# Two full products of the identity ahead of every second group's scores, in the context attention of the last two sequences

## The chip, the cores and the metric

The kernel runs on one core of a Trainium2 chip, in one launch. The metric is the device time of that launch in microseconds. Three runs of the kernel before gave 906.14, 907.43 and 909.11; the median is 907.43.

Five engines work side by side, each through its own list of instructions in order: TensorE (PE in the profile; its weight loads stand apart as PEld), VectorE (DVE), ScalarE (ACT), GpSimd (POOL) and SyncE (SP), which mostly issues transfers. They wait for each other by semaphores.

## The reference, cut to what matters

A decoder of two layers works on `x` of 4 sequences by 256 tokens by 256 channels. The six parts are added to `x` one after the other: latent attention, an attention over a context, a routed block, an attention over heads, the causal context attention that the change touches, and a mixture of 28 experts of which each token takes six. The part in question, and what follows it:

```python
def _L1_xattn_ref(q, latent_kv, Wq, Wkv_expand, Wout):   # 16 heads of 16
    qp = q @ Wq.T
    kv = latent_kv @ Wkv_expand.T
    k, v = jnp.split(kv, 2, axis=-1)
    ...
    scores = jnp.einsum('bhqd,bhkd->bhqk', qh, kh) * inv_sqrt_d
    scores = jnp.where(causal, scores, jnp.finfo(scores.dtype).min)
    attn = jax.nn.softmax(scores, axis=-1)
    out = jnp.einsum('bhqk,bhkd->bhqd', attn, vh)
    ...
    return out @ Wout.T
...
x = x + _L1_xattn_ref(_layernorm(x, axis=-1), ctx_512, ...)
x = x + _L1_ffn_ref(_layernorm(x, axis=-1), ...)
```

## The kernel before

All data is f32 but for some constants. A kernel-wide PSUM pool has three tags of two buffers each: `sc` (two banks a buffer), `tp` and `o`.

`_cross_attention` handles the sequences in two halves, `half(0)` for sequences 0 and 1 and `half(1)` for sequences 2 and 3. The second half runs alone on the core's engines but for the routing of the experts; the first runs beside the head attention. `front` makes the queries `f["qT"]` of two sequences at once: 128 rows (eight heads of 16, in two interleaved sets), two sets `g`, 512 tokens. A product of 128x512 (`xpq`, L1669) fills each set, and DVE scales it into `xqT` (L1670).

Each sequence `b` then has eight groups of two times one head: `g` (0, 1), `e` (0, 1), `sp` (0, 1). For a group, `scores` (L1545) takes a buffer of `sc` and fills its two banks. Each bank gets a product of 32 rows by 256 keys (`Q1`, the later queries), one of 32 rows by 128 keys (`Q0`), and then a product of the identity in bf16 with the mask (L1559). The first product into a bank is the one with `start=True`. DVE takes the maxima (`cnm`, L1561 and L1562), ACT the exponentials (`xpr`, L1567).

The groups are pipelined: when a group's scores are issued, `after` takes up the group two before it. `turned` transposes its exponentials, six times 128x128 into two `tp` tiles (`x_tp`), which DVE copies out (L1583), or ACT for the last of each four (L1581). With the next group's scores the sums over the values follow (`values`, `xav`: 128 rows by 32 columns, four side by side). After four groups `finish` scales the sums (`xwide` on ACT L1603, `xr_tp` on PE, `xrT` on ACT L1609, `xaT` on DVE L1611), and after eight it projects them (`xpo`, eight records of 128x256) and adds them to `x` (L1623).

Then `env["then"](b)` routes the sequence's tokens: statistics (L143 to L146), the reciprocal root on POOL (`ln_rs`, L135), the normed rows `R` (L151), their transposes `g_tp` (L630) and copy `ghT` (L632), the gate's product `pl` (L637), a chain of small DVE instructions to the chosen experts `gt` (L670), the ranks (`rank`, L677 and L678), the row numbers `rows` (L686), and twelve scatters from POOL into the `lists` in DRAM (L702). Steps of this alternate with the groups of the next sequence. POOL does all this in order: `R`'s clearing (L620) and the `ln_rs` of the next routing stand behind the twelve scatters.

The order of the PE instructions of this part is written out by a helper: `_InOrder` (`pe`) ties each product of line 94 and each transpose of line 97 to the one before it. Where the routing's own PE instructions (`g_tp`, `pl`, `rank`) stand among them, and the order on DVE and ACT, is left to a scheduler, which places them by its own estimates of time. So a change of one product can move others.

When the last `xpo` is done, the memory of this part is free, and the load of the experts' second weights (`wdn_e`, L593) starts into it; the experts follow.

Of the kernel before, what the change touches and what calls it, by code (L numbers as in the profile page):

```python
# [1481 lines left out]
def _cross_attention(nc, tc, x, w, env):  # L1482
# [5 lines left out]
    ident, identb, maskb, ln_apply, transposed = (env[n] for n in ("ident", "identb", "maskb", "ln_apply", "transposed"))  # L1488
    H = D = 16
    pe = _InOrder(nc, tc)  # L1490
# [53 lines left out]

    def scores(f, b, g, e, sp, ss):  # L1545
        sc = psum.tile([P, 2, 512], F32, tag="sc", name="xsc")
        t0 = b % 2 * S
        for cols, q0, n in ((Q1, P, S), (Q0, 0, P)):
            for j in range(2):
                rows = slice(32 * (2 * sp + j), 32 * (2 * sp + j) + 32)  # L1550
                pe.matmul(
                    sc[:, j, cols],
                    f["qT"][rows, g, t0 + q0 : t0 + q0 + P],
                    f["kz"][rows, e, g, t0 : t0 + n],
                    start=(n == S),
                    stop=False,
                )
        for j in range(2):
            pe.matmul(sc[:, j, P : 3 * P], identb, masks, start=False, stop=True)  # L1559
        nm = sm.tile([P, 2, 2], F32, tag="cnm", name="cnm")  # L1560
        nc.vector.tensor_reduce(nm[:, 1], sc[:, :, Q1], AX.X, ALU.max, negate=True)  # L1561
        nc.vector.tensor_reduce(nm[:, 0], sc[:, :, Q0], AX.X, ALU.max, negate=True)  # L1562
        pr = c3.tile([P, 2, 3 * P], F32, tag="xpr", name="xpr")
        for j in range(2):
            h = 8 * g + 2 * (2 * sp + j) + e
            for i, cols in ((1, Q1), (0, Q0)):
                nc.scalar.activation(  # L1567
                    pr[:, j, cols], sc[:, j, cols], AF.Exp, bias=nm[:, i, j : j + 1], accum_out=ss[:, i, h : h + 1]
                )
        return pr  # L1570
# [103 lines left out]
    def half(bp):  # L1674
        while bp not in kvs:
            yield
        f = yield from front(bp, kvs[bp])
        for b in (2 * bp, 2 * bp + 1):
            ss = c2.tile([P, 2, H], F32, tag="xss2", name="xss2")
            for n in range(8):  # L1680
                g, e, sp = n // 4, n // 2 % 2, n % 2
                now = (f, b, g, e, sp, scores(f, b, g, e, sp, ss), ss)
                yield
                advance()
                waiting.append(now)
                if len(waiting) > 2:
                    after(*waiting.pop(0))
                if b == B - 1:
                    advance()
                yield  # L1690
        if bp == 1:
            while waiting:
                after(*waiting.pop(0))
            state.pop("values")()
            while steps:
                advance()
# [121 lines left out]
```

## Time and profile before

| | us |
|---|---|
| median of three runs | 907.43 |
| the profiled execution | 933.27 |
| its span, first to last instruction | 931.5 |
| mean granted TensorE clock over the span | 0.837 of full speed |
| context attention of sequences 2 and 3, first scores to last `xpo` | 605.2 to 708.7 |
| PE busy in it | 78.6 of 103.5 |
| mean granted clock in it | 0.72 |

A row of the profile gives the busy time of a group of like instructions, and the idle time of its engine just before them with what ended it. A f32 product of the program stands in the trace as two records, a transpose as one. Ends of PE records are modelled. The granted clock (PEclk) is the share of full speed at which the TensorE array runs; the stretches by time give it for any piece of the span. "remote" marks a wait of which the profile finds no releaser among this core's instructions.

### The profile page before, as it was taken

To read this page: it belongs to the slowest core of one execution; us is meant where nothing else is said; L and a number is where in the kernel's file an instruction comes from. 1 tells how busy PE (TensorE), PEld (TensorE's weight loads), DVE (VectorE), ACT (ScalarE), POOL (GpSimd) and SP (SyncE) were. 2 spreads that over 40 slices of the span, in tenths; PEclk is the share of its full clock that TensorE was granted. 3 is DMA by queue.
4 is the path that set the end of the run, shared out by engine and by line. 5 is a ranking of instruction groups with operands and counts; after the bars stand their busy time and mean duration, and the time that the engine had idled before them with its cause. 6 is when DMAs were issued, how large, how long until landed. Compare 5 with 4: busy or idle time off the path is not lost.

```text
span 931.5 us, 11640 instructions
## 1 busy us (share of the span) xinstructions
PE 716.2 (77%) x3634; PEld 447.2 (48%) x3634; DVE 533.2 (57%) x1310; ACT 291.9 (31%) x962; POOL 310.3 (33%) x248
## 2 busy tenths in 40 slices
PE   4998999789988667334857778879665689969990
PEld 2555656445555333322423445556443357747770
DVE  3367457886553599878278579537334233353332
ACT  1245343442441302210322334235220234424440
POOL 2022122213210283440430330231440456645662
PEclk9899989889998588567866778869766799989995
DMA  8779999400515103110400000480124767685655
GB/s 314 206 236 325 325 326 327 180 1 0 181 37 190 47 1 107 73 46 16 137 0 1 1 1 1 184 326 14 64 75 100 230 104 128 111 213 87 112 77 154
DMA packets 85168, 117.83 MB, mean 126 GB/s; under 512 B 5774, under 2 KB 72975, under 8 KB 84594
## 3 DMA queue, kind: packets, MB, share of 16 engines
q1 hardware_dynamic: 72210, 100.26, 33.1%
q0 software_dynamic: 11232, 15.21, 9.7%
q10 hardware_dynamic: 1664, 1.57, 0.5%
q8 instruction: 33, 0.54, 0.2%
q14 instruction: 29, 0.24, 0.1%
HBM read 59.60 MB, written 55.33 MB: 123 GB/s over the span
## 4 chain that ended last, share of the span: by engine, by line
PE 38%; DVE 25%; DMA 14%; POOL 8%; issue 6%; ACT 6%; another core or an unknown queue 1%; SPq 1%; ACTq 0%; DVEq 0%; POOLq 0%
DMA acc<-ys,xb 10%; POOL qk L1412 5%; ACT pr L324 4%; PE xsc L94 3%; PE pgu L848 3%; PE po L94 2%; DVE pv L1437 2%; PE x_tp L97 2%; PE pq L94 2%; DVE s L1418 2%; DVE pr L333 2%; PE pqkv L1394 2%; PE av L94 2%; PE py L879 2%; DVE O L1444 2%
## 5 line engine op out<-in xcount | busy, mean ns | idle before, releaser
L884 POOL DMA_INDIRECT acc<-ys,xb x62 | 98.3, 1586 | 73.6 <-ACT Tx L840 48.0
L1412 POOL TENSOR_TENSOR qk<-qkv 128x1024 f32<-128x1024 f32 x32 | 74.2, 2349 | 92.2 <-ACT qkv L1398 92.2
L848 PE MATMUL pgu<-wgu_e,Tx 128*128 x248 | 90.8, 491 | 8.1 <-issue 6.8
L334 POOL TENSOR_TENSOR pr<-pr,rs 128x512 f32<-128x512 f32 x32 | 41.5, 1297 | 165.0 <-DVE rs L332 78.8
L324 ACT ACTIVATE pr<-sc,nb 128x256 f32<-128x256 f32 x128 | 58.9, 473 | 61.6 <-DVE nb L319 61.5
L1567 ACT ACTIVATE xpr<-xsc,cnm 128x256 f32<-128x256 f32 (+1 forms) x128 | 52.0, 422 | 65.3 <-DVE cnm L1562 50.3
L702 POOL DMA_INDIRECT lists<-R,rows x48 | 46.6, 971 | 59.4 <-DVE rows L686 19.1
L879 PE MATMUL py<-wdn_e,Th 88*128 x248 | 64.3, 385 | 0.8 <-DVE Th L861 0.5
L1418 DVE TENSOR_REDUCE s<-qk 128x128 f32<-128x2048 f32 x16 | 36.5, 2283 | 39.5 <-POOL qk L1412 39.5
L848 PEld LDWEIGHTS pgu<-wgu_e,Tx 128*128 128x128 f32 x248 | 44.3, 199 | 25.4 <-issue 11.1
L879 PEld LDWEIGHTS py<-wdn_e,Th 88*128 88x128 f32 x248 | 47.3, 193 | 17.2 <-DVE Th L861 1.1
L854 DVE TENSOR_TENSOR eh<-pgu,sg 128x176 f32<-128x176 f32 x62 | 21.1, 340 | 53.5 <-issue 31.8
L97 PE MATMUL x_tp<-cst,xpr 128*128 128x128 f32 x192 | 39.7, 345 | 12.5 <-DVE cnt L753 4.3
L94 PE MATMUL av<-pT,ckt 128*64 128x256 f32 x256 | 40.1, 408 | 10.1 <-DVE pT L350 9.9
L315 DVE TENSOR_REDUCE nm<-sc 128x4 f32<-128x1024 f32 x32 | 39.0, 1218 | 14.4 <-PE sc L94 14.3
L852 ACT ACTIVATE sg<-pgu 128x176 f32<-128x176 f32 x62 | 19.7, 317 | 78.4 <-PE pgu L848 68.1
L883 ACT ACTIVATE ys<-py,wsel 128x256 f32<-128x256 f32 x62 | 29.4, 473 | 38.6 <-PE py L879 33.6
L94 PE MATMUL sc<-ckv,qk 64*128 64x256 f32 x256 | 39.9, 413 | 1.5 <-ACT qk L302 0.7
L97 PE MATMUL tp<-cst,pr 128*128 128x128 f32 x256 | 38.1, 290 | 3.3 <-DVE pT L350 2.4
L94 PE MATMUL xsc<-kz,xqT 32*128 32x256 f32 (+1 forms) x256 | 38.5, 412 | 2.7 <-ACT xpr L1567 2.7
L868 DVE SCALAR_TENSOR_TENSOR wjunk<-cst,e_all,xb 128x28 f32<-128x28 f32 x62 | 15.3, 247 | 41.4 <-ACT ys L883 36.7
L97 PEld LDWEIGHTS x_tp<-cst,xpr 128*128 128x128 f32 x192 | 27.6, 176 | 22.0 <-issue 9.0
(339 smaller groups left out, 1523.7 us busy)
## 6 DMA issues: line engine op xcount, KB each, us to landing
lists<-blank SPq DMA_DIRECT2D x9, 3600.0 KB
wgu_e<-in_e_gu_dram SPq DMA_DIRECT2D x4, 2464.0 KB
xb<-lists SPq DMA_DIRECT2D x62, 144.0 KB
acc<-blank SPq DMA_DIRECT2D x5, 1152.0 KB
wdn_e<-in_e_dn_dram SPq DMA_DIRECT2D x4, 1232.0 KB
wq<-in_m_wq_dram SPq DMA_DIRECT2D x4, 1024.0 KB
mwo<-in_m_wo_dram SPq DMA_DIRECT2D x2, 2048.0 KB
part<-acc SPq DMA_DIRECT2D x16, 256.0 KB
```

The lines of the kernel that those rows point to most:

```text
L94: self._next(self.engine.matmul(*args, **kw))
L97: self._next(self.engine.transpose(*args, **kw))
L315: nc.vector.tensor_reduce(nm, sc, AX.X, ALU.max, negate=True)
L324: nc.scalar.activation(pr[:, e, qt, :], sc[:, e, qt, :], AF.Exp, bias=nb[:, e, qt : qt + 1], accum_out=ss[:, e, qt : qt + 1],)
L334: nc.gpsimd.tensor_tensor(pr[:, 1], pr[:, 1], rs[:, 1].unsqueeze(2).to_broadcast([P, 2, S]), ALU.mult)
L702: put = nc.gpsimd.indirect_dma_start(out=lists, out_offset=bass.IndirectOffsetOnAxis(ap=rows[:, i, n : n + 1], axis=0), in_=R[:, i, :], in ...
L848: nc.tensor.matmul(pg, xT[:, k, :], self.wgu[:, bass.ds(e * (4 * M) + k * 2 * M, 2 * M)], start=(k == 0), stop=(k == 1))
L879: nc.tensor.matmul(py, hT[:, k, :], self.wdn[:, bass.ds(e * (2 * C) + k * C, C)], start=(k == 0), stop=(k == 1))
L884: nc.gpsimd.indirect_dma_start(out=accs[self.puts % len(accs)], out_offset=bass.IndirectOffsetOnAxis(ap=xb[:, C : C + 1].bitcast(I32), axi ...
L1412: nc.gpsimd.tensor_tensor(pr[:, 4 * i : 4 * i + 4], q3[:, h0 : h0 + 4].unsqueeze(2).to_broadcast([P, 4, H, D]), k3.unsqueeze(1).to_broadca ...
L1418: nc.vector.tensor_reduce(s[:, hh], pr, AX.X, ALU.add)
L1567: nc.scalar.activation(pr[:, j, cols], sc[:, j, cols], AF.Exp, bias=nm[:, i, j : j + 1], accum_out=ss[:, i, h : h + 1])
```

## The change

Two products are added at the head of `scores`, for sequences 2 and 3 and for the groups with `sp == 0`, so for eight of the sixteen groups. Each multiplies the f32 identity (128x128) with all of `f["qT"][:, 0]` (128x512) and writes one of the two banks of the group's `sc` buffer. The scores' own first product into each bank begins with `start=True`, so that what the added products left there is overwritten and not read.

```diff
     def scores(f, b, g, e, sp, ss):
         sc = psum.tile([P, 2, 512], F32, tag="sc", name="xsc")
+        if b >= 2 and sp == 0:
+
+            for j in range(2):
+                pe.matmul(sc[:, j], ident, f["qT"][:, 0], start=True, stop=True)
         t0 = b % 2 * S
         for cols, q0, n in ((Q1, P, S), (Q0, 0, P)):
             for j in range(2):
```

All lines after it move down by four (L1561 becomes L1565, and so on). The scheduler's order changes in a few places with it. On PE, in the routing of sequence 1, three of the four `rank` products move up, ahead of the sums over the values (`xav`) and of three transposes; in the routing of sequence 2, the four `g_tp` transposes move up, ahead of sixteen `xav` records and six `x_tp`. On DVE a few instructions of these two routings change places with `cnm` and with one reciprocal (L1601), and on ACT one `xwide` comes earlier. POOL's and SP's orders are the same.

## The prediction

> **What bounds the kernel now.** I read the page first, then the stretches by time, then the chain of waits, then the order of time on TensorE and GpSimd. The page:
>
> ```profile
> span 931.5 us, 11640 instructions
> PE 716.2 (77%) x3634; PEld 447.2 (48%) x3634; DVE 533.2 (57%) x1310; ACT 291.9 (31%) x962; POOL 310.3 (33%) x248
> PEclk9899989889998588567866778869766799989995
> ```
>
> No engine is full over the span, and the granted clock has a trough in the middle (slices of 23.3 us each). The products that the change repeats stand at line 94, writing `xsc`; the groups of the last two sequences run from 605.2 to 708.7 us. Cut where the granted clock switches (columns: length, busy time of PE, PEld, DVE, ACT, POOL, then PEclk, DMA share, GB/s):
>
> ```profile
> 605.20:611.00 5.80, 4.05 (x43) 2.65 (x42) 1.71 (x3) 1.72 (x8) 4.30 (x5) 1.00 1.03 408
> 611.00:617.70 6.70, 4.56 (x20) 2.50 (x20) 1.12 (x2) 0.00 (x0) 3.84 (x4) 0.50 1.04 411
> 617.70:631.50 13.80, 12.62 (x56) 8.49 (x54) 6.53 (x14) 8.28 (x36) 0.26 (x3) 0.50 0.48 188
> 631.50:648.20 16.70, 15.49 (x153) 11.60 (x153) 14.25 (x53) 8.53 (x37) 0.72 (x1) 1.00 0.00 1
> 648.20:655.40 7.20, 4.92 (x51) 3.41 (x50) 3.62 (x7) 3.90 (x17) 5.65 (x6) 1.00 0.29 104
> 658.80:665.60 6.80, 2.69 (x22) 1.58 (x20) 1.13 (x3) 1.72 (x9) 3.75 (x7) 1.00 0.28 101
> 665.60:686.10 20.50, 16.90 (x85) 11.71 (x86) 11.43 (x47) 6.34 (x27) 3.38 (x4) 0.50 0.04 16
> 692.90:706.60 13.70, 8.79 (x48) 4.39 (x48) 3.40 (x16) 3.35 (x12) 3.84 (x4) 0.50 0.15 54
> ```
>
> The clock is 1.00 or 0.50 and nothing between. In the full-speed stretch 631.5 to 648.2, PE is busy 15.49 of 16.70 us: there TensorE is the bound, with 1.2 us to spare. Elsewhere it idles. Two things hold the order of the stage. One is GpSimd: each sequence's routing issues twelve scatters (L702), and the next routing's `ln_rs` (L135) is queued on POOL behind them:
>
> ```profile
> 662.24 0.96 POOL L702 DMA_INDIRECT lists<-R,rows  x1 [0.30 <-issue]
> 664.81 0.10 POOL L620 MEMSET R<- 128x6 f32 x1 [1.61 <-DMA lists<-R,rows]
> 668.37 0.72 POOL L135 TENSOR_TENSOR ln_rs<-ln_ve,neghalf 128x2 f32<-128x2 f32 x1 [3.29 <-DVE ln_ve L146]
> ```
>
> The batches start at 648.2 and 682.8 us, and twelve scatters take 12 x 1.265 = 15.2 us. The other thing is PE itself. At the end, the chain of waits runs through the last `xpo` straight into the load of the expert weights, so whatever ends the stage later ends the kernel later:
>
> ```profile
> 707.16 1.51 PE xpo L94 x6
> 708.68 12.05 DMA wdn_e<-in_e_dn_dram
> ```
>
> One feature of the profile needs care. Late in each batch VectorE waits for products that had ended long before, with no releaser found:
>
> ```profile
> DVE cnt L753 <- remote: 7.9, 1, 7.9
> DVE xpT L1583 <- remote: 5.7, 3, 4.4
> DVE x_in L1623 <- remote: 4.0, 1, 4.0
> ```
>
> The profiled execution took 933.27 us (931.5 of span, 1.8 around it); the median is 907.43, shorter by 25.8. These waits, ACT's like them, and another such stretch near 732 to 742 us sum to about that. My inference, not shown: they are mostly absent from the timed runs. So I make the sum twice, with them and without.
>
> **The change part by part.** It adds, before the scores of groups 0, 2, 4, 6 of both sequences, two products of 128*128 by 512 f32: eight pairs. Nothing is removed. The nearest row is the query product of the same shape:
>
> ```profile
> 599.12 6.19 PE L1669 MATMUL xpq<-hT,wxq 128*128 128x512 f32 x8
> ```
>
> Eight records are four program products; they start 0.855 us apart at clock 0.50. A pair is four records: 3.42 us at half clock, 1.71 at full (the scores block beside it takes 2.12 against 1.18). Eight pairs: 13.7 us at full, 27.4 at half. The identity's weight loads run beside the products (PEld 335 ns under 855) and cost nothing; if that cover went, 4 x 0.34 a pair. DVE, ACT, POOL and SP get no instruction. The pair takes over the score bank, so the wait for the group before last's exponentials moves from the first score to the pair; these end 1 to 2 us earlier, so I take 0, at most 1 us where ACT lags.
>
> What the pairs do to the clock: the switches (597.4, 604.2, 611.0, 631.5, 655.4, 658.8, 665.6, 686.1, 692.9, 706.6) lie on a grid of 3.41 us. [...] Here the Trainium skill speaks: "TensorE: Matmul & The Clock Gate", "What's actually happening", has about 3.4 us of sustained PE activity restore the clock. The trace differs: from 621.2 to 628.1 PE is busy all the time (3.40 of 3.40 us in each of two windows), in narrow scores and transposes, and the clock stays 0.50 until `xpo` has filled a window. By the page the clock would be back by about 623 unaided and the pairs would be pure cost; by the trace a pair at half clock fills a whole window and restores it, worth up to half of the PE work behind it: 6.3 us in the stretch 617.7 to 631.5. I use the trace.
>
> *Start of the stage to the batch at 648.2:* five pairs. With the late waits as profiled: PE idles 3.9 us before 617.7, which hides the first two pairs; the second restores the clock near 617.9, so 12.6 us of work shrinks by 6.3, less the third pair's 1.7 and about 1 us of DVE latency: -3.6. The fourth and fifth fall in the full-speed stretch: 3.4 less 1.2 idle, +2.2. Sum -1.4. Without the late waits: PE has work from 605 on, never falls to half for long, and the five pairs are 8.5 us on a nearly full engine, less 2 us of idle and 1 us for a half-speed window shortened: +5.5. I take +5.5.
>
> *Batch of 648.2 to that of 682.8:* the two pairs fall under the scatters; PE idles 6.4 us from 648.2 to 665.6 (2.3 and 4.1), so 0. If POOL's 15.2 us were gone, they would cost 3.4. The scheduler also moves instructions: the four `g_tp` transposes (L630), which wait for `R` behind POOL's `ln_rs`, now stand ahead of sixteen `xav` records and six `x_tp`, where before twelve `xav` ran at 666.77 first. These (1.5 and 1.4 us at half clock) now come between `g_tp` and `pl`, while DVE copies `ghT` (0.69): 0 to +1.5, I take +0.5. The earlier routing's `rank` products move ahead of `xav` as well and make PE wait for `gt` (DVE's chain from `lg` to `gt` took 3.7 us); it brings `rows` forward and `xav` back: -1 to +1, taken 0. No DMA and no scatter changes its place in a queue.
>
> *Batch of 682.8 to the end:* one pair, 1.7 to 3.4. Credit: it can bring full clock to what follows; PE does 8.8 us at half between 692.9 and 706.6, but in the profile the wait to 699.9 comes first and the clock falls again. Between -3 and +3.4, taken +0.5.
>
> Sum: 5.5 + 0.5 + 0.5 = +6.5 us, 913.9.
>
> **The rivals.** *Faster:* one mechanism, the clock. If the timed runs fall to half as in the profile, the pairs restore it: -1.4 in the first part, and in the last a pair at 681 that keeps full clock through 706 gives up to -3; sum -4.4, 903. It decides once more than 20 us of half-clock PE work on the path turns full: a us saved needs two, and some 10 us of the pairs are exposed. For it: 58 of the 103.5 us at half clock. Against it: between 617.7 and 648.2 the path is PE in both states, and only half of the low stretches lie there. *No change:* all pairs fall in waits, as with the first two and the sixth and seventh: 907.4. For it: 25 us of PE idle. Against it: the full-speed stretch has 1.2. *Much slower:* pairs run at half clock and the clock doesn't hold, because a wait over 3.4 us follows: six exposed pairs at about 2.5 us, +15, 922. *The pairs don't raise the clock at all*: 10 us exposed, +10, 917.5; unlikely, as `xpq` of the same shape did.
>
> **How the numbers follow.** A measurement of this kernel tells about 0.3% from no change, 2.7 us. Forecast (+3 to +10): 0.58. Faster, under -2.7: 0.16. Within: 0.12. Over +10 (both slow rivals): 0.14. The range from 903.5 (about the faster rival's own time) to 918.5 leaves out about 0.1 on each side; the forecast's own is 910.5 to 917.5. Slower: 0.58 + 0.14 = 0.72.
>
> **What would show it.** Right: 32 more `xsc` records of 128x512, near 430 ns apart where the clock is 1.00; a mean clock in 605 to 710 above the 0.72 of now; PE busier than before between 605 and 650; the second batch of scatters later by some us relative to the first. Wrong: the second batch starts at 645 or earlier (the clock was worth more), or at the same 648 with the pairs in former idle time. If `g_tp` no longer gates and `pl` runs at once, the part after 648 was mis-sized.

## The result, and the profile after

The changed kernel took 916.9 us (median of four runs, 914.57 to 923.28), the kernel before 908.27 beside it (906.14 to 909.27). The ratio is 1.010, with a 95% interval of 1.0061 to 1.014: slower by 8.6 us, between 5.5 and 12.7.

The two profiles seem to say the opposite: the span of the changed kernel is 914.6 us, that of the kernel before 931.5. The profiled executions are not alike. That of the changed kernel took 916.4 us, as its other runs did; that of the kernel before took 933.27, 25 us over its own median. Later runs of the kernel before had medians of 911 on one chip and of 932 to 936 on three others, and no execution of the one was as long as the shortest of the others. So the time goes by the chip, as far as these runs tell: each chip was used at one time only. A total time is compared below only with one from the same chip and time.

The page of the changed kernel: span, busy time of the engines, granted clock in 40 slices.

```profile
span 914.6 us, 11704 instructions
PE 720.5 (79%) x3666; PEld 448.7 (49%) x3666; DVE 534.2 (58%) x1310; ACT 292.3 (32%) x962; POOL 309.9 (34%) x248
PEclk9899999979999578767677776989876889979995
```

Its stretches from the first pair to the last `xpo`, cut at the batches of scatters and at the switches of the clock (length, busy time of PE, PEld, DVE, ACT, POOL, then PEclk, DMA share, GB/s; one stretch of 1.70 us is left out):

```profile
604.90:641.50 36.60, 35.99 (x290) 23.50 (x289) 24.38 (x73) 18.76 (x81) 9.05 (x13) 1.00 0.54 211
641.50:658.40 16.90, 11.94 (x82) 7.36 (x79) 7.25 (x19) 6.66 (x28) 11.92 (x16) 1.00 0.30 106
658.40:673.80 15.40, 13.49 (x60) 9.59 (x61) 8.25 (x35) 4.17 (x18) 0.66 (x1) 0.50 0.00 1
675.50:689.70 14.20, 13.22 (x113) 8.15 (x112) 8.55 (x31) 5.36 (x21) 10.23 (x11) 1.00 0.35 123
```

Up to the second batch, at 641.5, TensorE is busy for 35.99 of 36.60 us, all at full clock. In the profile of before, the same part held a late wait (one marked "remote") and a half-speed stretch; here is neither, and the list of waits has no line without a releaser. So this profile shows the second of the two cases for which the prediction made its sum. A pair in it, by the order of time on PE (start, duration):

```profile
604.77 1.88 PE L94 MATMUL xsc<-xqT,cst 128*128 128x512 f32 x4
606.59 0.92 PE L94 MATMUL xsc<-kz,xqT 32*128 32x256 f32 x8
```

From the pair's start to the first score it is 1.82 us. Behind the second batch, by the order of time on POOL and on PE:

```profile
658.34 0.72 POOL L135 TENSOR_TENSOR ln_rs<-ln_ve,neghalf 128x2 f32<-128x2 f32 x1
...
659.65 1.08 PE L630 MATMUL g_tp<-cst,R 128*128 128x128 f32 x4 [5.89 <-DVE R L151]
...
673.82 1.05 POOL L702 DMA_INDIRECT lists<-R,rows  x1 [14.76 <-DVE rows L686]
```

TensorE has run out of work, two pairs included, and waits 5.89 us for `R`, which hangs on POOL. The clock falls to half at 658.4, and `g_tp`, now ahead of `xav`, and all behind it run at half until 675.5. The chain that ended last again leads through the last `xpo` into the load of the expert weights:

```profile
688.10 1.58 PE xpo L94 x6
689.69 11.06 DMA wdn_e<-in_e_dn_dram
```

### The profile page after: what moved, and what is told of

It is laid out like the page before. It is cut to its first block, busy times and chain, and to the rows that moved or that the text cites. A ratio compares the mean times of both kernels' runs of the same rounds, so it can differ in the third digit from the quotient of the medians.

```text
span 914.6 us, 11704 instructions
## 1 busy us (share of the span) xinstructions
PE 720.5 (79%) x3666; PEld 448.7 (49%) x3666; DVE 534.2 (58%) x1310; ACT 292.3 (32%) x962; POOL 309.9 (34%) x248
## 4 chain that ended last, share of the span: by engine, by line
PE 39%; DVE 24%; DMA 13%; POOL 9%; ACT 7%; issue 6%; SPq 1%; ACTq 0%; DVEq 0%; POOLq 0%
DMA acc<-ys,xb 9%; POOL qk L1412 5%; ACT pr L324 4%; PE xsc L94 4%; PE pgu L848 4%; PE po L94 2%; DVE pv L1437 2%; PE py L879 2%; POOL lists L702 2%; PE pq L94 2%; DVE s L1418 2%; DVE pr L333 2%; PE pqkv L1394 2%; PE av L94 2%; DVE O L1444 2%
## 5 line engine op out<-in xcount | busy, mean ns | idle before, releaser
L848 PE MATMUL pgu<-wgu_e,Tx 128*128 x248 | 93.6, 503 | 2.9 <-ACT Tx L840 1.6
L879 PE MATMUL py<-wdn_e,Th 88*128 x248 | 66.2, 394 | 8.7 <-DMA wdn_e<-in_e_dn_dram 8.2
L879 PEld LDWEIGHTS py<-wdn_e,Th 88*128 88x128 f32 x248 | 48.8, 199 | 25.6 <-DMA wdn_e<-in_e_dn_dram 8.4
L97 PE MATMUL x_tp<-cst,xpr 128*128 128x128 f32 x192 | 35.3, 320 | 4.2 <-DVE xpT L1587 3.4
L94 PE MATMUL xsc<-kz,xqT 32*128 32x256 f32 (+1 forms) x256 | 36.3, 392 | 2.7 <-ACT xpr L1571 2.7
L97 PEld LDWEIGHTS tp<-cst,pr 128*128 128x128 f32 x256 | 29.2, 147 | 17.4 <-issue 14.1
```

The costliest lines, as they stand in the source:

```text
L94: self._next(self.engine.matmul(*args, **kw))
L97: self._next(self.engine.transpose(*args, **kw))
L848: nc.tensor.matmul(pg, xT[:, k, :], self.wgu[:, bass.ds(e * (4 * M) + k * 2 * M, 2 * M)], start=(k == 0), stop=(k == 1))
L879: nc.tensor.matmul(py, hT[:, k, :], self.wdn[:, bass.ds(e * (2 * C) + k * C, C)], start=(k == 0), stop=(k == 1))
```

## The experiments

Edits of the condition or of the products are shown against the changed kernel, that of the scatters against the kernel before, each cut to the lines that change.

**Are the late waits part of the kernel?** The kernel before, unchanged, profiled twice more, on two chips.

> The kernel before, unchanged, profiled a second time. What is to be seen is whether the late waits of its first profile (7.9 + 5.7 + 4.0 us on VectorE with no releaser found) belong to the kernel. If they were a feature of one execution, as the prediction inferred: they are gone here, the span is 905 to 908 us, the second batch of scatters starts near 633 (the changed kernel's 641.5 less five pairs of 1.8 us, plus what TensorE idles) and the last output product ends near 681. If they belong to the kernel: the span is again 925 to 933, the second batch starts near 648, and the changed kernel's profile, which shows none, has removed them.

Measured: 944.99 us, beside a median of 931.7 for the same kernel. The waits are there, in another mixture (list of waits of this run):

```profile
DVE xpT L1583 <- remote: 13.2, 5, 4.5
ACT xpT L1581 <- remote: 5.4, 1, 5.4
```

> The kernel before, unchanged, once more. Its second profile took 944.99 us and showed the late waits again, beside a median of 931.7 there and of 908.3 in the runs beside the changed kernel: so they are no feature of one execution. If they go with the times (an execution near 908 has none, one near 931 has them): here the profile shows whichever belongs to its own time. In a profile near 908, without them, the second batch of scatters should start near 633, the third 31 us later (18.1 from the batch to g_tp as in the changed kernel, 13.2 from g_tp to the next batch as with the old order), and the last output product should end near 681. In one near 931: second batch near 648 to 656, end near 708 to 717.

Measured: 930.72 us beside a median of 935.8, again with late waits (6.6, 6.1 and 5.4 us on VectorE), second batch at 646.87, last `xpo` to 706.2. Neither guess of the first expectation was right. The waits are not an accident of one execution, nor do they belong to the kernel everywhere. They go with the time: no kernel with all its scatters shows one in this part at a span of 914.6 us or less, and all of them do from 925 up.

**The change in halves**, on the chip with 931.7.

```diff
-        if b >= 2 and sp == 0:
+        if b == 2 and sp == 0:
```

> The pairs of sequence 2 only (four pairs); the order on all engines is that of the kernel before, but for the pairs. The prediction's sum: all four lie ahead of the second batch of scatters on a nearly full TensorE, 4 x 1.8 = 7.2 us less about 2 us of idle time: +4 to +6 us, ratio 1.005 to 1.006. If the cost of the change lies in sequence 3 and in the new order (g_tp at the head of TensorE's queue while it waits for GpSimd): 0 to +1 us.

Measured: 934.80 us, ratio 1.0038 (1.0017 to 1.0059), +3.5 us. This is just below the expected +4 to +6, whose greater part lies inside the interval (1.6 to 5.5).

```diff
-        if b >= 2 and sp == 0:
+        if b == 3 and sp == 0:
```

> The pairs of sequence 3 only (four pairs), which bring all of the changed order of the scheduler with them. The prediction's sum: one pair ahead of the second batch (+1.8), two hidden under the scatters (0), the new order +0.5, the last pair +0.5: +2 to +3.5 us, ratio 1.002 to 1.004. If the new order is what costs (TensorE stands 5.9 us before g_tp in the profile of the changed kernel): +5 to +8 us. If the parts add, this run and the one with sequence 2 only sum to the change's own +8.

Measured: 933.21 us, ratio 1.0011 (0.9973 to 1.0049): +1.0, not separated from no change. The new order does not cost 5 us or more: the upper bound is 4.6 for order and pairs together.

**The changed kernel where there are late waits**, on the chip with 935.8.

> The changed kernel, unchanged, beside more runs of the kernel before. The two sums of the prediction for the part before the second batch: -1.4 us with the late waits, +5.5 without. So where the kernel before takes 908 us: +8 to +9 as measured, ratio 1.009. Where it takes 931 us: the two halves measured alone there gave +3.5 and +1.0, so +2 to +5 if they add, ratio 1.002 to 1.005. A rival, that the change costs the same TensorE time either way: +8 in both.

Measured: 936.89 us, ratio 1.0014 (0.9993 to 1.0035): +1.3 us, and no change within its interval, where the chip of the result had +8.6 (ratio 1.0061 and up). So the same pairs have two prices. The stretches of this run from the first batch to the second, and those of the kernel before on the same chip (its third profile):

```profile
601.04:615.05 14.01, 10.46 (x53) 4.96 (x51) 2.41 (x4) 1.72 (x8) 10.84 (x11) 0.87 1.03 405
615.05:621.88 6.83, 3.22 (x9) 2.18 (x10) 2.42 (x5) 1.64 (x8) 1.22 (x4) 0.50 1.04 408
621.88:651.36 29.48, 28.87 (x236) 19.19 (x235) 20.19 (x65) 15.33 (x68) 0.72 (x2) 1.00 0.10 37
```

```profile
603.58:614.29 10.71, 8.79 (x49) 4.25 (x47) 2.41 (x4) 1.72 (x8) 8.27 (x9) 0.82 1.04 404
614.29:624.53 10.24, 6.30 (x36) 4.26 (x37) 3.59 (x7) 3.16 (x14) 3.79 (x7) 0.50 1.04 409
624.53:646.87 22.34, 20.98 (x192) 15.74 (x191) 18.36 (x63) 13.69 (x60) 0.72 (x2) 1.00 0.13 48
```

In the changed kernel TensorE waits for 7.17 us and loses the clock. The second pair is almost the first thing behind the wait, and the half-speed stretch lasts 6.83 us, as it does with the pairs of sequence 2 alone. In the five profiles with late waits and without a pair there it lasts 10.24 us (twice) or 20.48 (three times). So the clock does come back sooner with pairs. But the part is not shorter for it: 50.32 us from batch to batch, against 43.29 in the kernel before on this chip, and 47.60 and 50.64 in its other two profiles. Single executions with late waits differ here by about as much as five pairs cost. Why the medians on this chip are nearly the same is therefore not shown.

**What the pairs' use of the array is worth.** The eight pairs cut to a sixteenth of the array, with as many columns of data (on the chip with 931.7):

```diff
-                pe.matmul(sc[:, j], ident, f["qT"][:, 0], start=True, stop=True)
+                pe.matmul(sc[:32, j], ident[:32, :32], f["qT"][:32, 0], start=True, stop=True)
```

> All eight pairs, each product cut to 32 rows by 32 columns of the array, with the same 512 columns of data: the same time on TensorE at the same clock, a sixteenth of the array; the order on every engine is that of the changed kernel. If the pairs are plain TensorE time and the rest of the work holds the clock by itself: same as the changed kernel, +8 us, ratio 1.009. If the full products earn part of their price back by holding the clock (the prediction took a credit of 1 us in the part before the second batch, and none to 3 us at the end): +9 to +12 us, with more time at half clock between 604 and 690. If the full products carry the clock of the whole stage: +15 us or more.

Measured: 948.96 us, ratio 1.0196 (1.0146 to 1.0245), +17 us: the last of the three cases.

**Do the scatters make the late waits, and what does the change cost without them?** In the kernels before, changed and narrow, the scatters of three sequences are left out. POOL computes for as long in their place. The orders on TensorE, VectorE and ScalarE stay; the experts get fewer rows in the same blocks.

```diff
     for n in range(TOPK):
         if b < B - 1 and n:
             yield
+        if b < B - 1:
+            if n == 0:
+                nc.gpsimd.tensor_copy(R[:, :, :TOPK].bitcast(I32), rows)
+            for _ in range(20 * (n == 0)):
+                nc.gpsimd.tensor_tensor(R[:, 0, :2], ones[:, :2], env["neghalf"][:, :2], ALU.pow)
+            continue
```

> The kernel before without the scatters of sequences 0, 1 and 2 (their list entries are left out, so the experts get fewer rows in the same blocks): in the place of each batch of twelve stand, in the same place of POOL's order, a copy of the row numbers and twenty small powers of 0.72 us each, about 15 us as before. The orders of TensorE, VectorE and ScalarE are unchanged. If the late waits come with the scatters' transfers: no wait without a releaser is left between 600 and 715, and where the kernel before takes 931 this takes 905 to 912. Second batch near 633, last output product near 681. If they have another cause: they stay, and so does the time, within 3 us.

> The kernel before without the scatters of sequences 0, 1 and 2 (left out as in the first run of this), again; that run stood beside a kernel before of 910.6 us, without late waits, and told nothing of their cause. If the kernel before takes about 931 here, with late waits: 905 to 912 for this one if the scatters' transfers make the waits, 925 and more if not. If it takes about 908 here: -5 us again, as then (905.0 to 910.6), which is the 1.6 us of waiting for the last scatter in each of the batches and no more of the question.

Measured: first 905.03 us where the kernel before took 910.62 (0.9949, 0.9924 to 0.9974). That chip shows no late waits, so this run could not say what makes them. Then, on a chip where the kernel before took 934.97, 904.44 us: 0.9702 (0.9646 to 0.9759), 28 us less by the ratio and 30.5 by the medians. Some 5 us of that the edit is worth without late waits too, as on the first chip. The waits are gone from this part; what remains in the list stands beside the fourth batch, whose scatters were left in. The longest (in these kernels all lines after the edit stand six lower, `Th` included):

```profile
DVE Th L867 <- remote: 4.3, 1, 4.3
```

So the late waits come from the scatters, not from POOL being occupied. Nor are they due to traffic as such: in the place of the first batch other transfers kept the queues as full in this run as in those with late waits, and no wait came of it:

```profile
605.85:619.50 13.65, 13.51 (x114) 8.76 (x113) 8.78 (x17) 6.99 (x30) 12.26 (x20) 0.93 1.03 397
```

Whether it is the scatters' own transfers or the way in which POOL issues them was not separated.

> The changed kernel with the same replacement. Measured against the run before it, the change's cost without late waits. By the prediction's sum: +6.5 us (+5.5 up to the second batch, +0.5, +0.5); by the measured result, +8.6. If the changed kernel costs +1.4 as in the runs with late waits, whatever the waits: 0 to +3.

Measured: 911.46 us, on the chip of the first run: +6.4 over its 905.03. This is the cleanest pair of profiles, since both are free of late waits. Each is cut from the last four `xpq` records to the second batch of POOL work. The kernel before without scatters:

```profile
603.75:635.43 31.68, 30.37 (x271) 21.32 (x270) 24.26 (x73) 18.61 (x81) 13.09 (x22) 0.97 0.58 222
```

The changed kernel without scatters:

```profile
605.93:645.11 39.18, 38.57 (x292) 24.57 (x291) 25.00 (x73) 18.73 (x81) 13.09 (x22) 0.98 0.47 179
```

The part grows by 7.5 us, PE's busy time by 8.2, its idle time falls from 1.31 to 0.61. Nearly all of the idle time that there was to fill before is in three waits, from the list of waits on PE in this part:

```profile
PE x_tp L97 <- ACT xrT L1615: 0.5, 1, 0.5
PE g_tp L630 <- DVE R L151: 0.4, 1, 0.4
PE x_tp L97 <- DVE ghT L632: 0.2, 1, 0.2
```

> The same replacement, and the eight pairs cut to 32 rows by 32 columns of the array (same time on TensorE at the same clock). With late waits these narrow pairs cost 16 us more than the full ones. If that is the clock that full products bring back after a late wait, and without late waits TensorE never falls to half before the second batch: within 3 us of the full pairs without scatters, up to the second batch the same to 1 us. If the full products hold the clock in any case: +10 us and more over them.

Measured: 921.27 us, 9.8 more than with the full pairs, and 16.2 over the kernel before without scatters. The expectation of "within 3 us" fell. The stretch to the second batch, and the products themselves beside the full ones of the changed kernel (durations min/median/max in ns):

```profile
603.02:647.77 44.75, 44.14 (x285) 25.92 (x285) 25.18 (x73) 18.73 (x81) 13.09 (x22) 0.84 0.41 158
```

```profile
L94 PE MATMUL xsc<-xqT,cst x32: 587/600/1058, 605.8 to 679.2; 32*32 32x512 f32 x32
L94 PE MATMUL xsc<-xqT,cst x32: 592/592/1061, 604.8 to 674.8; 128*128 128x512 f32 x32
```

At full clock a narrow record takes 0.60 us, against 0.59 for a full one: as said, the same time. TensorE is busy for 44.14 of 44.75 us, and yet the clock goes to half, from 622.0 to 625.4 and again from 639.0 on. The kernel before without scatters holds full clock from 605.4 to 649.8 with no pairs at all. So narrow products do not leave the clock as it was; by taking TensorE's time with little of its array they lose it.

**One pair alone**, the second of the eight, on the chip with 910.6.

```diff
-        if b >= 2 and sp == 0:
+        if b == 2 and g == 0 and e == 1 and sp == 0:
```

> One pair alone, ahead of the third group of sequence 2 (the second of the eight); all orders as in the kernel before, the scatters as they are. With the late wait that ends near 618 this pair is the first full product behind it. By the prediction's sum with late waits it brings the clock back near 622 instead of 631, and is worth up to half of the half-speed work behind it less its own time: -6.3 + 1.7 at best, so -2 to -5 us where the kernel before takes 931. If the pair is only time on TensorE: +1.8 at full clock, +3.4 at half. Where the kernel before takes 908: +1 to +2.

Measured: 912.35 us, ratio 1.002 (1.0000 to 1.0041): +1.7, the price of one pair on a full engine, as expected for a chip without late waits. What this one pair brings with late waits was not tried. Its profile is of use besides: it has no late waits, the scatters are in, and the order is that of the kernel before. Two groups of scores, by their starts on PE, in the kernel before without scatters (4.61 us apart) and in this run, with the pair between them (6.32):

```profile
606.40 0.92 PE L94 MATMUL xsc<-kz,xqT 32*128 32x256 f32 x8
611.01 0.92 PE L94 MATMUL xsc<-kz,xqT 32*128 32x256 f32 x8
```

```profile
607.47 0.92 PE L94 MATMUL xsc<-kz,xqT 32*128 32x256 f32 x8
613.79 0.92 PE L94 MATMUL xsc<-kz,xqT 32*128 32x256 f32 x8
```

**Pairs only where TensorE waits anyway.** Four pairs ahead of the fifth group of sequence 3, none elsewhere.

```diff
-        if b >= 2 and sp == 0:
+        if b == 3 and g == 1 and e == 0 and sp == 0:
 
-            for j in range(2):
+            for j in (0, 1, 0, 1, 0, 1, 0, 1):
```

> Four pairs at one place only: ahead of the fifth group of sequence 3, the last scores before TensorE waits for R behind the second batch of scatters (7 to 9 us of waiting without pairs, of which four pairs at 1.81 fill 7.2); no pair elsewhere. The order of g_tp is that of the changed kernel, the rest that of the kernel before. If pairs under that wait cost nothing, and hold the clock for what comes after it (g_tp, pl, rank and the part after the third batch ran at half clock in the kernels with few pairs): the way from R to the third batch 1 us shorter in spite of the new order, the part after it 1 to 1.5 us shorter: -1 to -3 us, ratio 0.997 to 0.999. If the clock is lost in the waits that remain: +1 us, for the new order. If the pairs run past the wait: up to +4.

Measured, on the chip with 934.97: 930.83 us, ratio of the runs 0.998 (0.9959 to 1.0002), 2 us less by the ratio, 4 by the medians, and not separated from no change. The mechanism shows all the same. On PE in this run:

```profile
657.00 7.03 PE L94 MATMUL xsc<-xqT,cst 128*128 128x512 f32 x16
...
666.64 0.67 PE L630 MATMUL g_tp<-cst,R 128*128 128x128 f32 x4 [1.43 <-DVE R L151]
```

In the run with one pair the same engine waits, and finds half the clock behind the wait (two `g_tp` records take 0.66 us there, four 0.67 above):

```profile
656.68 0.66 PE L630 MATMUL g_tp<-cst,R 128*128 128x128 f32 x2 [8.48 <-DVE R L151]
```

With the four pairs in the wait the clock holds until 673.3, and the way from `g_tp` to the third batch takes 10.3 us (666.64 to 676.95) instead of 13.15, which it takes in the run with one pair and in all three profiles of the kernel before. Part of the gain is then lost: the clock falls before that batch, and the last part takes 25.6 us with its own late waits, as in the first profile of before (25.8). Whether this version is faster than the kernel before is open, and on a chip without late waits it was not run.

## Why the prediction was right, and where its sum was off

The sum without late waits was taken, +6.5, and the result is +8.6. The parts, from profiles without late waits (us; the first part begins with the last four `xpq` records):

| | to the second batch | to the third | to the last `xpo` |
|---|---|---|---|
| before, without scatters | 31.68 | 29.76 | 15.46 |
| changed, without scatters | 39.18 | 28.35 | 16.60 |
| one pair | 33.62 | 31.31 | 16.04 |
| changed | 39.21 | 32.31 | 15.84 |

- *Which execution the median stands for.* The prediction inferred that the late waits are mostly absent from the timed runs. Right: the changed kernel's profile at its median has none. What parts the timed runs from the profile was not known to the prediction: as far as these runs tell, the chip.
- *Start to the second batch, +5.5.* It was +7.5. The price of a pair was right: from score to score a pair adds 1.71 us in the run with one pair and 1.71 to 1.72 three times in the kernels without scatters, as forecast. (From its start to the first score it is 1.82, but the transposes ahead of it are followed 0.09 us sooner.) Five pairs at this price are about 8.6 us. The credits were mis-sized. The idle time to fill was put at 2 us; 0.7 of 1.3 was filled. The half-speed window that they were to shorten (1 us) does not exist without late waits: the clock is 1.00 from 605.4 to 649.8 in the kernel before without scatters. The new order, "-1 to +1, taken 0", gave 0.2: from the first `rank` product to the batch 3.68 us (641.43 to 645.11) after 3.88 (631.55 to 635.43). The `rank` products end sooner there, but VectorE then waits 0.68 us for the transposes that now stand behind them, ahead of `rows`.
- *Second batch to third, +0.5.* The pairs cost nothing there, as said: 5.89 us of waiting are left. The order of `g_tp` costs what was bounded: from `g_tp` to the third batch 14.17 us (659.65 to 673.82) against 13.15 with the old order (656.68 to 669.83, both at half clock), +1.0 in a range of 0 to +1.5. Without scatters the part is 1.4 shorter in the changed kernel; there the clock came back between, from 665.8 to 669.2, which the prediction did not count.
- *Third batch to the end, +0.5 between -3 and +3.4.* With scatters -0.2 against the run with one pair: the last pair runs at half clock, 3.49 us from 672.28, and the clock is full from 675.5 on. Mean clock in this part 0.95 against 0.74. Without scatters +1.1.
- *Sum.* 7.5 + 1.0 - 0.2 = +8.3, against +8.6 measured. These parts come from different pairs of runs; the pair without scatters alone gives 7.5 - 1.4 + 1.1 = +7.2, where its medians differ by 6.4. That 8.3 is so near to 8.6 is in part luck.
- *The sum with late waits*, -1.4 + 0.5 + 0.5 = -0.4: measured +1.3 (-0.7 to +3.3) where the waits are, which fits, but its reason is not shown. The second pair does shorten the half-speed stretch, to 6.83 us. The part that was to be 1.4 us shorter is 7.0 longer than in the kernel before on the same chip, in single executions that differ by that much without pairs.
- *The other rivals.* Pairs at half clock: all up to the second batch ran at full. No change: not on the chip of the result. A faster kernel: shown on neither kind of chip. Pairs that do not raise the clock: with the last pair it is full 1.7 us after the start of the third batch, in the run with one pair 8.3 us after.
- *The clock rule.* The prediction set the trace against the Trainium skill, "TensorE: Matmul & The Clock Gate", "What's actually happening", where 3.4 us of sustained activity restore the clock. The narrow pairs are the test: busy 44.14 of 44.75 us, and the clock falls. It is the part of the array in use that counts in these runs; that is shown for 32x32 against 128x128, and how much of it is needed is open. In one point the prediction read its trace too narrowly: it let the clock wait for `xpo`. In the third profile of before it was back at 624.53, ahead of any `xpo`, `xpq` or pair, 5.4 us after TensorE took up steady work at 619.13.
- *The signs that it named.* The 32 records of the pairs are there, some 450 ns apart. The mean clock between 605 and 710 is 0.84 (0.72 before) and PE is busy for 44.07 us between 605 and 650 (38.72 before), as it said. But those compare executions with and without late waits. The second batch came at 641.5, under the 645 that it gave as a sign of being wrong, and 41.3 us after the first instead of more than 47.6: by the signs as written the prediction would have been called wrong. Between profiles that are both without late waits the sign holds: 33.9 us without scatters and pairs, 41.4 with pairs.

## What to carry to other kernels

Before two profiles are compared, hold each execution's own time against the median of its kernel; a gap of 25 us says that the profile shows another case than the times do, and then the sum must be made for both. Where executions differ by as much as the change costs, one profile of each does not show what the change did. Work that is added to keep TensorE's clock costs its full time on an engine that is already busy and warm (1.71 us a pair here); count the idle time there, wait by wait, before calling it hidden. Inside a wait, four pairs shortened the next step by 2.8 us, but no version here was shown to be faster as a whole. What is added must also use the array: narrow products of the same length cost 10 us more than full ones.

## What was unexpected of the hardware

The same program takes 908 to 911 us on some chips and 932 to 936 on others. The difference sits beside the twelve scatters from GpSimd: while they run, VectorE and ScalarE begin on TensorE's results long after these were done. In the changed kernel with late waits, `x_tp` ended at 610.3, the last scatter at 616.2 (615.23 and 0.96), and VectorE's copy of `x_tp` began at 618.05:

```profile
609.44 0.88 PE L97 MATMUL x_tp<-cst,xpr 128*128 128x128 f32 x6
618.05 1.02 DVE L1587 COPY xpT<-x_tp 128x384 f32<-128x384 f32 x2 [8.26 <-remote]
```

Without those scatters the time is 904 to 905 on either kind of chip, and POOL's work of the same length in their place does no harm. What holds VectorE back, and why only on some chips, no run here shows.
